# A decoder's closing branch: a hint on every engine ahead of it, the last layer norms inside its arms, the last reload summed by products

## The chip, the core and the metric

The kernel runs on one core of a Trainium2 chip: TensorE (PE, matrix products), VectorE (DVE), ScalarE (ACT), GpSimd (POOL) and SyncE (SP, which issues DMAs), each with its own instruction stream, and 16 DMA engines. The metric is the device time of one execution in microseconds (us). Times within a profile count from the span's first instruction.

## What is computed

Two decoder layers on x (4 batches of 256 tokens, 256 wide), in float32: windowed attention, attention over a context of 1601 rows, a ternary feed-forward, then a second attention, a linear attention, and a mixture of experts. Each step ends in a layer norm of the sum of its input and its outcome. The change lies in the last step:

```python
def _layernorm(x, axis=-1, eps=1e-05):
    m = jnp.mean(x, axis=axis, keepdims=True)
    v = jnp.var(x, axis=axis, keepdims=True)
    return (x - m) / jnp.sqrt(v + eps)
...
        for e in range(E):
            h = jax.nn.silu(x @ w1[e]) * (x @ w3[e])
            out = out + h @ w2[e] * weights[:, e:e + 1]
...
    x = _layernorm(x + _L1_ffn_ref(x, L1_ffn_w_gate, L1_ffn_w1, L1_ffn_w3, L1_ffn_w2), axis=-1)
```

Of the 8 experts each token uses its 2 best, so `weights` has two entries that are not zero in each of the 1024 rows.

## The kernel before, in words

**Order of the work.** The program is written as a graph of operations. A planner (`weave`, L319) walks through it with a cost for each operation and a delay between engines (L192), takes the operation that can start first (ties go by priority, then by order of creation), and so writes out each engine's stream. While `hold_order(True)` is in force (L208), that order is kept; an operation that switches it off leaves the order of its instructions to the scheduler of the language. Buffers come from rings of a fixed number of places, and an operation waits until its ring has one free.

**The experts.** Tokens are entered into lists by expert in DRAM, and the lists are worked off in tiles of 128 rows (`expert_tile`, L1436). SyncE loads the tile's row and its expert from a table `tab` into registers and fetches the rows (`xg`) and two weight matrices (`wt`, a ring of 4). TensorE transposes the rows, multiplies them by both weights (32 products) and by a third (8), and VectorE makes the outcome `ey`. Most tiles are scattered by GpSimd into the table `yd` in DRAM, a row for each token and rank. Tiles are worked off early where the routing so far allows it; 16 late ones are planned after the last routing, with a table of their own (`tile_table`, L1379). It also makes `enough`, a flag in SBUF that says whether 13 late tiles suffice (as they do here), or whether the 3 rare ones are needed too.

**The end.** Four banks in PSUM, `acc[b]`, hold a batch of 256 tokens each. The last two sure tiles aren't scattered: their rows are summed into `acc` by products with a matrix of ones and zeros (`pick`, one piece for each batch, L1504). After the first of the two, the loop at L1653 issues 8 reloads of `yd` (two for each batch, 256 KB each, `back`, a ring of 4 buffers). VectorE adds both to the batch's x (L1660), and TensorE adds x to `acc[b]` by a product with the identity (L1663). Then `norms` (L1514) does for each batch: statistics by VectorE (`st`, `mv`), the power -1/2 by GpSimd (`rstd`), the bias `nmr` and the outcome of the first 128 tokens (`o[:, 0]`) by VectorE. These stand in the planned order.

**The branch.** `end` (L1538) comes behind everything else. Each of the five engines loads `enough` into a register (L1556), and `tc.Switch` (L1557) makes two arms. Arm 1 is `leave` (L1533): ScalarE makes the outcome of the other 128 tokens of each batch and SyncE issues four output DMAs. Arm 0 works off the three rare tiles first, then does the norms again and leaves. Each arm begins with a hint for its own exit, which the language puts there (L1557 in the profile); the jump into the arm and the jump out of it are shown at L1733, as is the closing barrier. All engines but ScalarE and SyncE have nothing to do in arm 1. The loads of L1556 stand outside the kept order.

Of the kernel before, what the change touches and what calls it, by code (L numbers as in the profile page):

```python
# [23 lines left out]
F32 = mybir.dt.float32  # L24
# [22 lines left out]
class View:  # L47
# [138 lines left out]
class Loom:  # L186
# [66 lines left out]
    @contextmanager  # L253
    def piece(self, us, claims=(), ins=(), over=(), what=""):


        self.cur = ([], [], list(ins))
        yield
        fns, outs, ins = self.cur
        self.cur = None  # L260
        if self.at_once is not None:
            over = ()
        read = [o for v in over for _, o in v.buf.reads]
        self.op({"PE": (us, us, lambda: [f() for f in fns])}, outs, ins, claims, after=read, what=what)

    def mm(self, o, lhsT, rhs, start, stop, **kw):
        fns, outs, ins = self.cur
        outs.append(o)
        ins += [v for v in (lhsT, rhs) if isinstance(v, View)]
        fns.append(  # L270
            lambda: self.nc.tensor.matmul(real(o), real(lhsT), real(rhs), start=real(start), stop=stop, **kw)  # L271
        )
# [162 lines left out]
def decoder(ctx: ExitStack, tc: tile.TileContext, a: dict, out: bass.AP):  # L435
    nc = tc.nc
    k = Loom(tc)
    piece, mm, turn = k.piece, k.mm, k.turn


    def scope(side, after=(), on=None):
        s = Scope(k, side, after)
        if on:
            s.opened.deps.add(on.opened)
            on.closed.deps.add(s.closed)
        return s

    base = scope("left")
# [118 lines left out]
    ident = const.tile((P, P), F32, "ident")  # L567
# [43 lines left out]
    vs = []  # L611
    for i in range(2):
        v = p1w.tile((P, 3, H // 2, 2, 32), F32, f"v{i}")
# [624 lines left out]
    LATE = TILES - sum(EARLY)  # L1238
    LAST_TILES = 2
# [271 lines left out]
        k.vector.tensor_tensor(slots, slots, slot, ALU.add)  # L1511
        scatter(yd, slots, y, 1.0, 2.0, "give", cleared)

    def norms(acc):  # L1514

        parts = []
        for b in range(B):
            mv = tiny((P, 2, 2), "mv2")
            for t in range(2):
                st = tiny((P, 6), "st")  # L1520
                k.vector.bn_stats(st, acc[b][:, t, :])
                k.vector.bn_aggr(mv[:, t, :], st)
            rstd = tiny((P, 2), "rstd2")
            k.gpsimd.tensor_scalar(rstd, mv[:, :, 1], 1e-5, None, ALU.add)
            k.gpsimd.tensor_tensor(rstd, rstd, mhalf, ALU.pow)
            nmr = tiny((P, 1), "nmr")
            k.vector.scalar_tensor_tensor(nmr, mv[:, 1, 0:1], -1.0, rstd[:, 1:2], ALU.mult, ALU.mult)
            o = p6.tile((P, 2, D), F32, "back", bufs=4)
            k.vector.tensor_scalar(o[:, 0], acc[b][:, 0], mv[:, 0, 0:1], rstd[:, 0:1], ALU.subtract, ALU.mult)
            parts.append((o, rstd, nmr))  # L1530
        return parts

    def leave(acc, parts):  # L1533
        for b, (o, rstd, nmr) in enumerate(parts):
            k.scalar.activation(o[:, 1], acc[b][:, 1], AF.Identity, scale=rstd[:, 1:2], bias=nmr)
            k.dma_start(out[b * S : (b + 1) * S, :].rearrange("(t p) d -> p t d", p=P), o)

    def end(tiles, tab, enough, level, acc, parts):  # L1538

        spare = {}  # L1540
        for v in (
            p5.tile((P, W), F32, "xg"), p6w.tile((P, 2, 2, EI), F32, "wt"), p6.tile((P, 2, P), F32, "xgT"),
            p6.tile((P, EI // P, P), F32, "eh"), p6.tile((P, D), F32, "ey"), p5.tile((P, 1), F32, "of", bufs=2),
            p6.tile((P, T // P, P), F32, "pick", bufs=LAST_TILES), tiny((P, 2, 2), "mv2"), tiny((P, 6), "st"),
            bank((P, 2, P)), bank((P, EI // P, P)), bank((P, EI // P, P)), bank((P, D)),
        ):
            spare.setdefault(v.buf.group.tag, []).append(v)
        held = [v for vs in spare.values() for v in vs]
        for vs in parts:
            for v, tag in zip(vs, ("back", "rstd2", "nmr")):  # L1550
                spare.setdefault(tag, []).append(v)

        def emit():
            k.hold_order(False)
            engines = (nc.tensor, nc.vector, nc.gpsimd, nc.sync, nc.scalar)
            which = {e.engine: e.value_load(enough.real()[0:1, 0:1], min_val=0, max_val=1) for e in engines}  # L1556
            for arm in tc.Switch(which, 2):  # L1557
                k.at_once = spare
                if arm:
                    leave(acc, parts)  # L1560
                else:
                    for i in tiles:
                        expert_tile(i, tab, level, acc)
                    leave(acc, norms(acc))
                k.at_once = None
            k.hold_order(True)

        outs = [v for vs in parts for v in vs]
        k.op({None: (0.0, 2.5, emit)}, [*acc, *outs], [tab, enough, w2], held, after=[o for o in k.ops if o.bufs], unordered=True)


    for b in range(B):
# [45 lines left out]
    w2 = p6w.tile((P, NE, 4, D), F32, "w2e")  # L1618
    for e in range(NE):
        k.dma_start(w2[:, e], rows(a["w2"][e]))  # L1620
    level = 0
    for b in range(B):
        at_prio(7, b)
        for ts, x, xt in l1_attention(b):
# [5 lines left out]
            if b == B - 1:  # L1630
                at_prio(8)
                n = EARLY[ts[0]]
                tab, taken = tile_table(n, taken)
# [8 lines left out]
    tab, enough = tile_table(LATE, taken, True)  # L1642
    iotaT = p6.tile((P, T), F32, "iotaT", bufs=1)
    iota(iotaT, 1, base=1)
    acc = [bank((P, 2, D)) for _ in range(B)]
    sure = LATE - RARE
    for i in range(sure):
        last = i - sure + LAST_TILES
        if last < 0:
            expert_tile(i, tab, level)  # L1650
        else:
            expert_tile(i, tab, level, acc, last == 0)
        if last == 0:  # L1653
            for b in range(B):
                x = X[b]
                for e in range(2):
                    y = p6.tile((P, 2, D), F32, "back", bufs=4)
                    row0 = 1 + e * T + b * S
                    k.dma_start(y, yd[row0 : row0 + S, :].rearrange("(t p) d -> p t d", p=P))
                    k.vector.tensor_tensor(x, x, y, ALU.add)  # L1660
                with piece(0.87, what="base"):
                    for t in range(2):
                        mm(acc[b][:, t, :], ident, x[:, t, :], False, True, skip_group_check=True)  # L1663
    end(range(sure, LATE), tab, enough, level, acc, norms(acc))
    k.weave()


# [69 lines left out]
```

## Time and profile before

| what | value |
|---|---|
| runs | 687.3, 689.1, 689.75 us (median 689.1) |
| the profiled execution: its time, its span | 687.61 us, 685.9 us |
| TensorE (PE) busy | 653.6 us, 95% |
| VectorE, ScalarE, GpSimd busy | 443.6, 296.2, 121.0 us |
| mean granted TensorE clock | 0.991 |
| DMA | 85.37 MB, mean 124 GB/s |
| first reload issued, last reload issued | 659.36, 665.96 us |
| first output issued, last output issued | 674.34, 678.33 us |

The page gives the busy time of each engine; the timeline gives single instructions, with the idle time ahead of them and what ended it; the view of one source line gives shortest, median and longest of each kind of instruction there, with the first and the last start. A letter q behind an engine means its sequencer, which reads the stream and runs branches, register loads and waits itself. The trace has a record for each of these instructions; where a time below is given to the hundredth for one of them, it is from its record.

### The profile page before, as it was taken

Reading aid. Unit: us, or ns where it says so; the run is one execution under the profiler, and the core shown is the slowest. Engines: PE = TensorE matmul, PEld = TensorE weight load, DVE = VectorE, ACT = ScalarE, POOL = GpSimd, SP = SyncE. Lnnn points to the kernel's source line nnn. Section 1 sums busy time; section 2 is a strip of 40 time slices with the busy share of each in tenths; the row PEclk is TensorE's granted clock in tenths of the full one; section 3 lists DMA queues with packets and bytes.
Section 4 is the critical chain, followed back from the end, with each engine's and each line's share of the span. In section 5 each row is a group of like instructions: output and inputs, shape, how many; then the busy total and the mean of one; then the engine's idle time right before and its main releaser. Section 6 shows DMA issues by size and latency. Waiting matters only on the chain.

```text
span 685.9 us, 12319 instructions
## 1 busy us (share of the span) xinstructions
PE 653.6 (95%) x4389; PEld 521.0 (76%) x4389; DVE 443.6 (65%) x1152; ACT 296.2 (43%) x930; POOL 121.0 (18%) x166
## 2 busy tenths in 40 slices
PE   8999999999999999999999999999997899899992
PEld 6878788678877677777667677777765799899992
DVE  6899886433526845365599997777688466334344
ACT  4779766211132423334346777656455312111101
POOL 3331132122300000000022101141213222121102
PEclk9999999999999999999999999999999999999997
DMA  9932121527998423000010340000000681896442
GB/s 307 357 105 64 46 65 40 177 100 232 328 338 314 158 84 108 0 1 1 0 55 1 105 143 1 1 32 1 31 1 17 209 301 53 298 339 217 147 131 71
DMA packets 62464, 85.37 MB, mean 124 GB/s; under 512 B 4462, under 2 KB 45812, under 8 KB 62388
## 3 DMA queue, kind: packets, MB, share of 16 engines
q1 hardware_dynamic: 60756, 79.96, 35.3%
q0 software_dynamic: 1632, 4.48, 1.8%
q8 instruction: 39, 0.64, 0.4%
q14 instruction: 37, 0.30, 0.1%
HBM read 67.29 MB, written 17.13 MB: 123 GB/s over the span
## 4 chain that ended last, share of the span: by engine, by line
PE 78%; DVE 13%; ACT 4%; DMA 1%; issue 1%; POOL 1%; SPq 0%; DVEq 0%; POOLq 0%; ACTq 0%
PE bank L271 70%; PE bank L278 9%; DVE at L408 3%; ACT at L408 3%; DVE nm L408 2%; DVE x L408 1%; POOL rstd L408 1%; DVE as L408 1%; DVE h L408 1%; DMA wt<-in_w 1%; DVE st L408 1%; DMA back<-yd 1%; DVE entry L408 1%; DVE fm L408 0%; DVE hq L408 0%
## 5 line engine op out<-in xcount | busy, mean ns | idle before, releaser
L408 ACT ACTIVATE at<-at,nm 128x128 f32<-128x128 f32 (+1 forms) x256 | 106.4, 419 | 23.3 <-DVE nm L408 22.6
L271 PE MATMUL bank<-xgT,wt 128*128 128x128 f32 x640 | 75.9, 279 | 1.9 <-DMA wt<-in_w 1.4
L271 PEld LDWEIGHTS bank<-xgT,wt 128*128 128x128 f32 x640 | 75.1, 195 | 3.0 <-issue 1.7
L278 PE MATMUL bank<-ident,at 128*128 128x128 f32 (+1 forms) x440 | 60.8, 275 | 2.0 <-DVE at L408 1.8
L278 PEld LDWEIGHTS bank<-ident,at 128*128 128x128 f32 (+1 forms) x440 | 50.2, 141 | 13.8 <-issue 6.4
L271 PE MATMUL bank<-V,aT 128*128 128x256 f32 (+1 forms) x240 | 55.1, 380 | 0.6 <-DVE o L408 0.6
L271 PE MATMUL bank<-KT,qT 128*128 128x512 f32 (+1 forms) x128 | 54.7, 553 | 0.0
L271 PEld LDWEIGHTS bank<-V,aT 128*128 128x128 f32 (+1 forms) x240 | 45.2, 190 | 10.6 <-issue 3.6
L408 POOL TENSOR_SCALAR rstd<-mv 128x2 f32<-128x2 f32 (+1 forms) x26 | 5.8, 221 | 258.1 <-DVE mv L408 186.9
L271 PE MATMUL bank<-kf,V 128*128 128x256 f32 (+1 forms) x208 | 50.0, 381 | 1.1 <-DVE kf L408 1.1
L408 DVE TENSOR_REDUCE nm<-at 128x4 f32<-128x512 f32 (+1 forms) x64 | 50.6, 808 | 0.4
L271 PE MATMUL bank<-wkv,KT 128*128 128x256 f32 (+1 forms) x208 | 49.6, 382 | 0.0
L408 ACT ACTIVATION_READ_ACCUMULATOR at<-at,nm 128x1 f32 x256 | 48.6, 190 | 0.0
L271 PEld LDWEIGHTS bank<-kf,V 128*128 128x128 f32 (+1 forms) x208 | 38.5, 190 | 7.3 <-DVE kf L408 2.3
L271 PEld LDWEIGHTS bank<-wkv,KT 128*128 128x128 f32 (+1 forms) x208 | 37.9, 186 | 7.0 <-issue 1.0
L408 ACT COPY aT<-bank 128x512 f32<-128x512 f32 (+2 forms) x58 | 30.6, 554 | 26.6 <-PE bank L278 25.8
L408 ACT ACTIVATE eh<-bank 128x512 f32<-128x512 f32 x20 | 11.9, 597 | 68.6 <-PE bank L271 59.0
L408 DVE TENSOR_REDUCE m<-bank 128x1 f32<-128x512 f32 (+1 forms) x32 | 20.4, 639 | 29.7 <-PE bank L271 29.7
L408 DVE TENSOR_TENSOR at<-at,rs 128x512 f32<-128x512 f32 (+1 forms) x44 | 38.4, 872 | 1.0
L408 POOL TENSOR_TENSOR at<-at,rs 128x512 f32<-128x512 f32 (+1 forms) x20 | 22.8, 1142 | 87.5 <-DVE rs L408 80.3
L271 PE MATMUL bank<-w2e,eh 128*128 x160 | 37.8, 380 | 0.0
L408 ACT ACTIVATE fm<-bank 128x512 f32<-128x512 f32 (+2 forms) x33 | 17.9, 550 | 45.7 <-PE bank L271 45.2
(268 smaller groups left out, 1237.0 us busy)
## 6 DMA issues: line engine op xcount, KB each, us to landing
wt<-in_w SPq DMA_DIRECT2D x40, 512.0 KB
lists<-h SPq DMA_DIRECT2D x6, 1548.0 KB
KT<-in_ctxT SPq DMA_DIRECT2D x6, 1024.0 KB
V<-in_ctx SPq DMA_DIRECT2D x6, 1024.0 KB
w2e<-in_w SPq DMA_DIRECT2D x8, 512.0 KB
KT<-in_ctxT SPq DMA_DIRECT2D x6, 577.0 KB
V<-in_ctx SPq DMA_DIRECT2D x6, 512.0 KB
xg<-lists SPq DMA_DIRECT2D x20, 129.0 KB
```

Source lines behind the costliest of these rows:

```text
L271: lambda: self.nc.tensor.matmul(real(o), real(lhsT), real(rhs), start=real(start), stop=stop, **kw)
L278: fns.append(lambda: self.nc.tensor.transpose(real(o), real(x), real(ident)))
L408: return getattr(engine, method)(*[real(x) for x in args], **{k: real(x) for k, x in kw.items()})
```

## The change

There are three parts.

**A hint on every engine.** `tell` is a new operation. It loads `enough` into a register of each engine and issues a hint for the coming branch with it, in the kept order. It is created behind the second-last sure tile and may be planned as soon as that tile has been summed into `acc[0]`; it takes no time in the plan. `end` uses these registers.

**The norms in both arms.** `norms` and `leave` become one function, which both arms call. The statistics of batch b+1 now come ahead of `nmr` and the outcomes of batch b. ScalarE makes seven of the eight outcomes, VectorE the first one of the last batch. `nmr` is made for both halves in one instruction.

**The last reload.** For the last batch, x takes only the first of the two reloads; the second goes to `acc[3]` by products of its own.

```diff
-    def norms(acc):
-
-        parts = []
+    def leave(acc):
+
+        rest = []
+
+        def go(b, mv, rstd):
+            nmr = tiny((P, 2), "nmr")
+            k.vector.scalar_tensor_tensor(nmr, mv[:, :, 0], -1.0, rstd, ALU.mult, ALU.mult)
+            o = p6.tile((P, 2, D), F32, "back", bufs=4)
+            for t in range(2):
+                if t == 0 and b == B - 1:
+                    k.vector.tensor_scalar(o[:, t], acc[b][:, t], mv[:, t, 0:1], rstd[:, t : t + 1], ALU.subtract, ALU.mult)
+                else:
+                    k.scalar.activation(o[:, t], acc[b][:, t], AF.Identity, scale=rstd[:, t : t + 1], bias=nmr[:, t : t + 1])
+            k.dma_start(out[b * S : (b + 1) * S, :].rearrange("(t p) d -> p t d", p=P), o)
+
...
             k.gpsimd.tensor_tensor(rstd, rstd, mhalf, ALU.pow)
...
+            rest.append((b, mv, rstd))
+            if b:
+                go(*rest.pop(0))
+        go(*rest.pop(0))
+
+    def ask(enough):
+
+        engines = (nc.tensor, nc.vector, nc.gpsimd, nc.sync, nc.scalar)
+        return {e.engine: e.value_load(enough.real()[0:1, 0:1], min_val=0, max_val=1) for e in engines}
+
+    where = {}
+
+    def tell(enough, what):
+
+        def emit():
+            where.update(ask(enough))
+            tc.switch_hint(where, 2, "end")
+
+        k.op({None: (0.0, 0.1, emit)}, [], [enough, what], unordered=True)
...
         def emit():
             k.hold_order(False)
-            engines = (nc.tensor, nc.vector, nc.gpsimd, nc.sync, nc.scalar)
-            which = {e.engine: e.value_load(enough.real()[0:1, 0:1], min_val=0, max_val=1) for e in engines}
-            for arm in tc.Switch(which, 2):
+            for arm in tc.Switch(where, 2, "end"):
                 k.at_once = spare
-                if arm:
-                    leave(acc, parts)
-                else:
+                if not arm:
                     for i in tiles:
                         expert_tile(i, tab, level, acc)
-                    leave(acc, norms(acc))
+                leave(acc)
...
         if last == 0:
+            tell(enough, acc[0])
             for b in range(B):
                 x = X[b]
                 for e in range(2):
                     y = p6.tile((P, 2, D), F32, "back", bufs=4)
...
-                    k.vector.tensor_tensor(x, x, y, ALU.add)
-                with piece(0.87, what="base"):
-                    for t in range(2):
-                        mm(acc[b][:, t, :], ident, x[:, t, :], False, True, skip_group_check=True)
-    end(range(sure, LATE), tab, enough, level, acc, norms(acc))
+                    if e == 0 or b < B - 1:
+                        k.vector.tensor_tensor(x, x, y, ALU.add)
+                for v in (x,) if b < B - 1 else (x, y):
+                    with piece(0.87, what="base"):
+                        for t in range(2):
+                            mm(acc[b][:, t, :], ident, v[:, t, :], False, True, skip_group_check=True)
+    end(range(sure, LATE), tab, enough, level, acc)
```

More of the change, by code (lines that the diff above doesn't have):

```diff
@@ L1525, in norms, with end @@
             k.gpsimd.tensor_tensor(rstd, rstd, mhalf, ALU.pow)
[L1526 to L1538, printed above, removed]
+            rest.append((b, mv, rstd))
[11 more added lines that the diff above has]
+        k.op({None: (0.0, 0.1, emit)}, [], [enough, what], unordered=True)
+    def end(tiles, tab, enough, level, acc):
         spare = {}
@@ L1543, in end @@
             p6.tile((P, EI // P, P), F32, "eh"), p6.tile((P, D), F32, "ey"), p5.tile((P, 1), F32, "of", bufs=2),
-            p6.tile((P, T // P, P), F32, "pick", bufs=LAST_TILES), tiny((P, 2, 2), "mv2"), tiny((P, 6), "st"),
+            p6.tile((P, T // P, P), F32, "pick", bufs=LAST_TILES),
+            *[tiny((P, 2, 2), "mv2") for _ in range(4)], *[tiny((P, 6), "st") for _ in range(4)],
+            *[tiny((P, 2), "rstd2") for _ in range(4)], *[tiny((P, 2), "nmr") for _ in range(4)],
+            *[p6.tile((P, 2, D), F32, "back", bufs=4) for _ in range(4)],
             bank((P, 2, P)), bank((P, EI // P, P)), bank((P, EI // P, P)), bank((P, D)),
@@ L1548, in end @@
         held = [v for vs in spare.values() for v in vs]
-        for vs in parts:
-            for v, tag in zip(vs, ("back", "rstd2", "nmr")):
-                spare.setdefault(tag, []).append(v)
         def emit():
             k.hold_order(False)
-            engines = (nc.tensor, nc.vector, nc.gpsimd, nc.sync, nc.scalar)
-            which = {e.engine: e.value_load(enough.real()[0:1, 0:1], min_val=0, max_val=1) for e in engines}
-            for arm in tc.Switch(which, 2):
+            for arm in tc.Switch(where, 2, "end"):
                 k.at_once = spare
-                if arm:
-                    leave(acc, parts)
-                else:
+                if not arm:
                     for i in tiles:
                         expert_tile(i, tab, level, acc)
-                    leave(acc, norms(acc))
+                leave(acc)
                 k.at_once = None
             k.hold_order(True)
-        outs = [v for vs in parts for v in vs]
-        k.op({None: (0.0, 2.5, emit)}, [*acc, *outs], [tab, enough, w2], held, after=[o for o in k.ops if o.bufs], unordered=True)
+        k.op({None: (0.0, 2.5, emit)}, acc, [tab, enough, w2], held, after=[o for o in k.ops if o.bufs], unordered=True)
     for b in range(B):
```

## The prediction

> **What bounds the kernel now.** I read the page's chain first: TensorE holds 78% of the path to the end, VectorE 13%. The change touches only the last 27 us and one register load, so I went on to the branch's own records, the timeline of the tail, and the chain around that load.
>
> The records of the end of the program (min/median/max in ns, first and last start in us):
>
> ```profile
> L1733 SPq DRAIN  x3: 7/7/13, 681.2 to 685.3; - x3
> L1733 POOLq DRAIN  x3: 40/113/2927, 682.1 to 685.6; - x3
> L1733 ACTq COMPARE_BRANCH  x2: 43/50/58, 657.7 to 677.8; - x2
> ...
> L1733 PEldq COMPARE_BRANCH  x2: 3435/3989/4543, 671.1 to 675.0; - x2
> ...
> L1733 POOLq COMPARE_BRANCH  x2: 43/56/70, 676.5 to 679.5; - x2
> ...
> L1733 DVEq COMPARE_BRANCH  x2: 60/68/75, 677.3 to 680.4; - x2
> L1733 ACTq DRAIN  x2: 14/78/142, 678.2 to 685.3; - x2
> ...
> L1733 DVEq DRAIN  x2: 10/29/48, 683.0 to 685.4; - x2
> ```
>
> Each engine branches twice, into its arm and out of it. The arm's first instruction is this one:
>
> ```profile
> L1557 ACTq BRANCH_PREFETCH_HINT  x1: 46/46/46, 660.2 to 660.2; - x1
> ...
> L1557 POOLq BRANCH_PREFETCH_HINT  x1: 52/52/52, 679.3 to 679.3; - x1
> ...
> L1557 DVEq BRANCH_PREFETCH_HINT  x1: 61/61/61, 680.2 to 680.2; - x1
> ```
>
> GpSimd branches at 676.45 and is in its arm at 679.31: 2.86 us. It leaves at 679.50 and drains at 682.12: 2.62 us more. Its DRAIN then lasts 2.93 us, to 685.05, and the closing barrier starts from there and ends the span 0.8 us later. VectorE pays 2.93 and 2.53 us in the same way. ScalarE, which reached its arm at 660, leaves at 677.75 and drains at 678.20, so an exit hinted long before costs 0.45 us. SyncE has seen the last output land by 681.0 and drains at 681.25. So **two branches and a drain on an engine with no work left** end the program, 3.8 us after the data are out.
>
> The tail's own work (timeline, start and duration in us):
>
> ```profile
> 671.97 1.89 PE L271 MATMUL bank<-ey,pick 128*128 128x256 f32 x8
> ...
> 674.34 4.36 SPq L285 DMA_DIRECT2D out<-back  x4
> ...
> 677.04 0.16 DVE L408 SCALAR_TENSOR_TENSOR nmr<-mv,rstd 128x1 f32<-128x1 f32 x1 [0.37 <-POOL rstd L408]
> 677.12 0.54 DVE L408 TENSOR_SCALAR back<-bank,mv,rstd 128x256 f32<-128x256 f32 x1
> 677.74 0.56 ACT L408 ACTIVATE back<-bank,nmr,rstd 128x256 f32<-128x256 f32 x1 [0.42 <-DVE back L408]
> ```
>
> The last product ends at 673.86, the last outcome at 678.30; the last output is issued at 678.33 and lands by 681.0.
>
> Last, the chain of waits around the loads of `enough` (start, us, what):
>
> ```profile
> 581.54 0.55 DVEq L1556
> 582.09 0.08 issue
> 582.16 0.22 DVEq L1556
> ...
> 582.57 0.48 DVE ey L408
> ```
>
> ```profile
> 585.41 4.63 DMA wt<-in_w
> 590.04 0.14 issue
> 590.18 3.81 PE bank L271 x32
> ```
>
> Today's register loads were placed early in the instruction order, right behind `enough`. VectorE's stands in front of the outcome `ey`, which stands in front of `tab`, and SyncE needs `tab` to ask for the first late weights. No transfer runs until 585.4, and TensorE idles 1.36 us for them at 590.18.
>
> [...]
>
> **The change part by part.** Numbers are against the profiled execution (687.61 us, span 685.9).
>
> *Moving the loads.* The five loads leave the place above. VectorE's there is five waits, load, arithmetic and assert, 581.05 to 582.50. Without it `ey` starts when its products end (581.57) and the step before allows: 581.65, as `rowi` follows the same kind of step by 0.60 at 575.63. That is 582.57 - 581.65 = 0.9 us earlier for `tab`, SyncE's requests and the first weights, whose queue is empty till then. TensorE's idle 1.36 us covers it. From 594.7 on TensorE runs without a wait on transfers, so the gain stays. **-0.9 us**; bounds -1.36 (the whole idle time) and 0 (another input of that tile is late next).
>
> *The hint, with the loads in front of it.* The planner puts `tell` when the second-last sure tile has been summed into acc[0]. By the planned times of before that is behind VectorE's first reload sum, behind SyncE's first four reload issues, behind TensorE's second summing piece of that tile, and behind all other work of ScalarE and GpSimd. ScalarE and GpSimd wait there for 10 us, so it is free on them. SyncE issues its fourth reload by 661.3 and its fifth at 663.88, when the first buffer comes free: 2.6 us, against 0.54 for a load and its check (579.12 to 579.66) and some 0.3 for the hint: free. TensorE's sequencer is 2.7 us ahead of its array (branch read at 671.14, last product ends 673.86) and takes a 0.63 us load (592.71 to 593.34) without a gap: free; with that cover gone, 0.6. On VectorE it is not free. The sequencer starts at 663.19; the load with its waits is 1.45 us, the hint, an unseen form, is taken as a branch set-up (0.3 at 677.06 to 677.36) with its own 0.06: 1.8 us, to 665.0. The second sum could start at 663.88, so sums two to four are 1.1 us late (0.65 if the five waits go). Behind them queue the sixth to eighth reload, whose buffers they free, and TensorE's sums. The fifth, issued in time, no longer shares the rings, so I take **+0.6 us** for the products; bounds 0.2 and 1.1.
>
> *The last reload by products.* VectorE loses one sum (0.67 us, no longer last); TensorE gains one piece of four matmuls at 0.216 us, 0.86 us. By priority both pieces for b=3 now stand ahead of the last tile's sums for b=1 to 3. From the b=2 piece at 669.27: b=3 at 670.24 and 671.10, then summing at 671.97, 672.83 and 673.69. acc[1] is complete at 673.0 (before: 671.3), acc[3] at 674.7 (673.9).
>
> *The norms in the arm.* VectorE ends its sums at about 669.8 and dispatches. If the arm is there, it starts at 670.4 (+0.6) and norms b=0 before acc[1] is complete. One batch is 0.95 us of statistics (674.85 to 675.80); then GpSimd starts 0.2 later and takes 1.0 (676.00 to 677.01). Statistics of b=1 at 673.03, of b=2 at 674.05; nmr of b=1 waits for GpSimd till 675.22; statistics of b=3 from 675.30 to 676.25; GpSimd 676.45 to 677.46; nmr at 677.49, before 677.04. The outcome on VectorE and the one on ScalarE then need 0.56 side by side if ScalarE waits for nmr alone (end 678.25), or one after the other, as at 677.12 and 677.74 (end 678.75). Output issued at 678.3 to 678.75, before 678.33: 0 to +0.4, I take **+0.2 us**. ScalarE's seven at 0.56 fit in its 1.1 us per batch.
>
> *Leaving the arms.* GpSimd enters its arm while idle, hinted or not, and hints its exit 10 us ahead. After its last power at 678.06 (677.46 + 0.6) it should drain after 0.45, as ScalarE did, at 678.5; with the same 2.93, done at 681.4. VectorE is out by 680. TensorE has no work in the arm: even at its 4.54 it is in time. So the end goes to the output: SyncE's drain at 681.25 + 0.6 + 0.2 = 682.05, and the barrier follows. The slack of 685.05 - 681.25 = 3.8 is gone: **-3.8 us**. What is late next is the landing, with GpSimd's drain 0.65 us behind; without that cover each further 0.1 on GpSimd counts.
>
> **Sum:** -0.9 + 0.6 + 0.2 - 3.8 = -3.9 us. The span becomes 682.0, the profiled execution 683.7. It lies 1.5 below the median of 689.1, so I put the same 3.9 on the median: **685.2 us**. Its own range, from the bounds, is 684.2 to 686.6.
>
> **Rivals.** (B) *Cheaper:* five waits are dropped on VectorE and ScalarE waits for nmr alone: 0.2 and 0 in place of 0.6 and 0.2, so 684.6, or 684.1 with the whole idle time saved. For it: 0.9 us of cover before acc[1]. (C) *The exits still fetch:* GpSimd is done at 678.06, fetches 2.62 and drains 2.93: 683.6, against 685.05: -1.4 - 0.9 = -2.3, **686.8**. Against it: ScalarE's 0.45. (D) *The hint into the arm does nothing*, so the change doesn't do what it says: VectorE's arm starts at 673.9 and the statistics of b=1 at 674.9. GpSimd's power for b=0 then ends at 676.05 and holds nmr and the statistics of b=2 behind it; those of b=3 start at 677.27, nmr of b=3 at 679.4 in place of 678.1: +1.3, **686.5**. For it: no hint of this kind, from a register, is in the trace. (E) *Slower:* [...] At TensorE's dearest 4.54 us: 4.54 on the reload path and 4.54 - 2.2 at the arm, 6.9 in all: -3.9 + 6.9 = +3.0, **692.1**. [...] against it: about a dozen VectorE instructions lie between hint and branch.
>
> **How the numbers follow.** Forecast 0.55, B 0.14, C 0.11, D 0.15, E 0.05. Runs of before spread by 2.45 us, so I widen the outer cases by 1: 683.1 to 687.9. A measurement of this kernel tells about 0.5% (3.4 us, 685.7) from no change. Two thirds of the forecast, nearly all of B and a fifth of D lie below: faster 0.53; same 0.42; slower 0.05, from E.
>
> **What would show it.** After the change: no L1556-like load before `ey` near 581, and the first wt wait of TensorE 0.9 shorter; VectorE's hint into the arm within 0.5 us of its branch; GpSimd's drain starting below 679; SyncE's drain the last before the barrier, at about 682. A branch of VectorE or GpSimd followed by 2.5 us of nothing is D or C; a pause of that length between reload sums is E; GpSimd's long drain ending last would make the sum wrong.

## The result, and the profile after

| | before | after | after, measured again |
|---|---|---|---|
| median of the runs | 689.75 us | 687.11 us | 687.78 us (before beside it: 689.95) |
| lowest to highest | 687.3 to 690.98 | 684.19 to 687.74 | 684.75 to 689.08 |
| ratio to before, 95% interval | | 0.9956 (0.9938 to 0.9975) | 0.9970 (0.9952 to 0.9988) |
| profiled execution: time, span | 687.61, 685.9 us | 684.19, 682.4 us | span 685.5 us |

The change makes the kernel faster, by 2.6 us the first time and 2.2 the second, 0.4 and 0.3%. Predicted were 3.9 us. The profiled execution, against which the sum was made, gained 3.42 us in time and 3.52 in span (685.90 - 682.38). So there are two questions: whether the terms behind those 3.5 us are the predicted ones, and why the medians show about 1 us less.

**The end of the program.** In the kernel after, the loads of `enough` are at L1546, the hint for the branch at L1554, each arm's hint for its own exit at L1575, and the jumps and the closing barrier at L1751. The view of that last line (shortest/median/longest in ns, first and last start in us):

```profile
L1751 POOLq DRAIN  x3: 40/113/3190, 677.0 to 682.1; - x3
L1751 SPq DRAIN  x3: 7/7/13, 681.5 to 681.8; - x3
...
L1751 POOLq COMPARE_BRANCH  x2: 56/62/68, 655.6 to 676.5; - x2
...
L1751 DVEq COMPARE_BRANCH  x2: 63/73/83, 668.4 to 677.3; - x2
...
L1751 PEldq COMPARE_BRANCH  x2: 364/1833/3302, 669.9 to 674.0; - x2
...
L1751 DVEq DRAIN  x2: 19/54/90, 677.9 to 681.8; - x2
```

GpSimd leaves its arm at 676.53 and starts its long DRAIN at 676.97: 0.44 us, where it took 2.62. That DRAIN is as long as ever (3.19 us), but it is over at 680.16. SyncE has seen the last output land at 681.50, and the span ends 0.88 later. The end has gone from an idle engine to the output, as the sum said.

**The entries.** The hints for the branch, and the first instruction of each arm:

```profile
L1554 PEldq BRANCH_PREFETCH_HINT  x1: 53/53/53, 661.7 to 661.7; - x1
L1554 SPq BRANCH_PREFETCH_HINT  x1: 45/45/45, 661.7 to 661.7; - x1
...
L1554 DVEq BRANCH_PREFETCH_HINT  x1: 68/68/68, 663.8 to 663.8; - x1
```

```profile
L1575 SPq BRANCH_PREFETCH_HINT  x1: 36/36/36, 669.8 to 669.8; - x1
L1575 PEldq BRANCH_PREFETCH_HINT  x1: 36/36/36, 670.3 to 670.3; - x1
L1575 DVEq BRANCH_PREFETCH_HINT  x1: 45/45/45, 671.3 to 671.3; - x1
```

VectorE jumps at 668.36 and is in its arm at 671.27: 2.91 us, as without a hint (2.93). SyncE takes 3.20, ScalarE 3.27, GpSimd 2.81. TensorE alone jumps at 669.89 and is there at 670.32. **On four of five engines the hint into the arm saved nothing.** GpSimd's stands at 580.69, ahead of fourteen scatters; the prediction had put it behind all of that engine's other work. ScalarE's comes 0.26 us ahead of the jump, and there the jump even took longer: 3.2 to 3.3 us in the four profiles with this lead, 2.5 to 2.7 in the six with no hint or with a missed one 3.7 us or more ahead. ScalarE has 12 us to wait after it, so this costs nothing.

The prediction and the expectations speak of fetches. What a jump waits for isn't shown: while VectorE jumps (668.36 to 671.27), packets of the two instruction queues start at 669.40, 670.38 (8 KB each) and 671.02 (16 KB), but their records name no engine, so taking one for VectorE's, or for the cause of its wait, is a guess.

**The late weights.** What TensorE waited for between 575 and 600 us (total, times, longest), first from the list of before, then the whole list of after:

```profile
PE bank L271 <- DMA wt<-in_w: 1.4, 1, 1.4
```

```profile
PE bank L271 <- DVE xgT L408: 0.5, 1, 0.5
```

**The tail** (timeline: start and duration in us, idle time before in brackets):

```profile
663.97 2.62 DVE L408 TENSOR_TENSOR entry<-entry,back 128x512 f32<-128x512 f32 x4 [1.22 <-DMA back<-yd]
...
670.89 2.75 PE L271 MATMUL bank<-ey,pick 128*128 128x256 f32 x12
671.43 0.43 DVE L408 BATCH_NORM_STATS2 st<-bank 128x6 f32<-128x256 f32 x1 [2.61 <-PE bank L271]
...
675.09 3.96 SPq L285 DMA_DIRECT2D out<-back  x4
...
677.31 0.16 DVE L408 SCALAR_TENSOR_TENSOR nmr<-mv,rstd 128x2 f32<-128x2 f32 x1 [0.97 <-POOL rstd L408]
677.39 0.54 DVE L408 TENSOR_SCALAR back<-bank,mv,rstd 128x256 f32<-128x256 f32 x1
678.09 0.56 ACT L408 ACTIVATE back<-bank,nmr,rstd 128x256 f32<-128x256 f32 x1 [0.69 <-SPq L1751]
```

The 1.22 us ahead of the second sum hold the loads and the hint (VectorE's sequencer is at them from 661.95 to 663.85); the list puts them down to the reload, which had landed. The 2.61 ahead of the first statistics are put down to TensorE, but acc[0] had long been complete: they are the jump. These busy rows show no jump; the sequencer's records have it, at 668.36 and 671.27.

**An account that doesn't depend on the execution.** Executions differ by several us ahead of the tail, so I count the tail from the start of the last sure tile's outcome `ey` on VectorE. "Landing" is the time from the issue of the last output to SyncE's drain. All in us, one profile each. The two profiles of the kernel after differ by 0.27 in the last output and by 0.54 in the end, so a difference between two rows that is smaller than this says little by itself.

| kernel | `ey` at | VectorE jumps | is in its arm | last output issued | landing | end |
|---|---|---|---|---|---|---|
| before | 662.77 | 14.53 | 17.46 | 15.56 | 2.86 | 23.13 |
| after | 661.66 | 6.69 | 9.61 | 17.01 | 2.82 | 20.71 |
| after, again | 664.25 | 6.65 | 9.86 | 17.28 | 3.09 | 21.25 |
| e1 no hint | 662.67 | 6.24 | 9.34 | 16.83 | 4.27 | 22.01 |
| e2 loads moved alone | 661.93 | 14.58 | 17.81 | 15.61 | 3.43 | 24.66 |
| e3 norms in the arms alone | 667.13 | 6.87 | 9.99 | 17.35 | 3.78 | 22.04 |
| e4 hint 7 us earlier | 664.90 | 5.94 | 9.04 | 16.46 | 3.68 | 21.03 |
| e5 hint 81 us ahead | 664.56 | 6.79 | 7.39 | 16.27 | 3.40 | 20.56 |
| e6 hint 61 us ahead | 663.62 | 6.12 | 6.72 | 15.74 | 3.20 | 19.83 |
| e7 last reload summed | 665.81 | 7.23 | 10.17 | 17.51 | 2.94 | 21.35 |
| e8 last outcome split | 663.41 | 6.39 | 9.25 | 16.64 | 3.09 | 20.62 |
| e9a hint 22 us ahead | 662.97 | 5.62 | 8.71 | 16.10 | 3.52 | 20.49 |
| e9b hint 20 us ahead | 662.38 | 6.50 | 9.65 | 17.07 | 3.26 | 21.21 |
| e12 e6, order held | 662.20 | 5.86 | 6.46 | 15.17 | 4.15 | 20.20 |

The records of the granted TensorE clock fit most of the differences in `ey`. Between 300 and 600 us TensorE ran at full clock but for stretches of 3.4 us at half of it, in which it had work, and their number is not the same in each execution. With one stretch (before, after, e1, e2, e9a, e9b, e12) `ey` stands at 661.7 to 663.0, with two (after again, e4, e5, e6, e8) at 663.4 to 664.9, with three (e3, e7) at 665.8 and 667.1. Half of 3.4 us is 1.7 us lost for each, by estimate. The profiled executions of before and after have one each, so they can be compared.

For the profiled executions: `ey` is 1.1 us earlier, the last output comes 1.45 us later after it, the landing is the same, and from SyncE's drain to the end it is 0.88 in place of 4.71. Together -1.10 + 1.45 - 0.04 - 3.83 = -3.52.

### The profile page after: what moved, and what is told of

Read it like the earlier page. It is cut to its first block, busy times and chain, and to the rows that moved or that the text cites. A ratio compares the mean times of both kernels' runs of the same rounds, so it can differ in the third digit from the quotient of the medians.

```text
span 682.4 us, 12346 instructions
## 1 busy us (share of the span) xinstructions
PE 654.6 (96%) x4389; PEld 521.1 (76%) x4393; DVE 442.3 (65%) x1148; ACT 297.5 (44%) x933; POOL 121.1 (18%) x166
## 4 chain that ended last, share of the span: by engine, by line
PE 66%; DVE 14%; issue 11%; ACT 4%; POOL 3%; DMA 1%; DVEq 0%; POOLq 0%; SPq 0%; ACTq 0%
PE bank L271 57%; PE bank L278 8%; DVE at L408 4%; ACT at L408 3%; DVE nm L408 2%; POOL yd L1290 2%; DVE x L408 1%; DVE as L408 1%; DVE h L408 1%; DVE st L408 1%; DMA back<-yd 1%; POOL rstd L408 1%; DVE entry L408 0%; DVE fm L408 0%; DMA yd<-ey,slots 0%
## 5 line engine op out<-in xcount | busy, mean ns | idle before, releaser
L271 PE MATMUL bank<-xgT,wt 128*128 128x128 f32 x640 | 74.3, 275 | 0.7 <-DVE xgT L408 0.5
L271 PEld LDWEIGHTS bank<-xgT,wt 128*128 128x128 f32 x640 | 73.5, 192 | 1.8 <-DVE xgT L408 0.8
L408 POOL TENSOR_TENSOR at<-at,rs 128x512 f32<-128x512 f32 (+1 forms) x20 | 22.8, 1141 | 87.6 <-DVE rs L408 80.4
```

The costliest lines, as they stand in the source:

```text
L408: return getattr(engine, method)(*[real(x) for x in args], **{k: real(x) for k, x in kw.items()})
```

## The experiments

My theory after the result: moving the loads gives 1.1, the exits give 3.8, and 1.5 is given back because VectorE's arm is late and its norms are slower than planned; the hints, but for TensorE's, save nothing. Times below are medians, and each ratio is to the kernel before measured beside it. All kernels compute everything.

### The parts alone

**e1: no hint.**

```diff
-            tc.switch_hint(where, 2, "end")
...
-            for arm in tc.Switch(where, 2, "end"):
+            for arm in tc.Switch(where, 2):
```

> The kernel after without its hint; the five register loads stay at their new place. Theory (of the five entry hints only TensorE's does anything, and TensorE's jump is hidden): VectorE's jump into the arm still takes 2.8 us, TensorE's takes 3.4 to 4.5 us instead of 0.36 and moves nothing; VectorE's stop between the first two reload sums is 0.45 us shorter, which the landing of the sixth reload absorbs; outputs and the last drain within 0.3 us of the kernel after in a profile at the same clock (span 682.1 to 682.5 at a granted clock of 0.993), times equal within the interval. Rival (the hints help VectorE or SyncE, or TensorE's late jump holds the end): the last output is issued at least 0.8 us later, span 683.2 or more.

Measured: 687.11 us, ratio 0.9965 (0.9951 to 0.9979); the kernel after had 687.11. VectorE's jump took 3.10, TensorE's 3.75 into the arm and 4.56 out of it. The span (684.7) misses what I had written and would fit the rival, but only because `ey` came 1.0 us later and the landing took 4.27; after `ey` the last output is issued 0.2 us *earlier* than with the hint. So no gain is seen from the hint where the change puts it, and TensorE's jump, the one that it saves, is hidden. An expectation in absolute times was a mistake: from here on I read the tail from `ey`.

**e2: the loads moved, nothing else.**

```diff
+            tell(enough, acc[0])
...
-            which = {e.engine: e.value_load(enough.real()[0:1, 0:1], min_val=0, max_val=1) for e in engines}
-            for arm in tc.Switch(which, 2):
+            for arm in tc.Switch(where, 2):
```

(`tell` holds the five loads here, and no hint.)

> The kernel before with one edit: the five register loads are issued in the kept order, behind the second-last sure tile's first summing. No hint, norms ahead of the branch as before. Theory (the move is worth 1.1 us and nothing else): the wait of TensorE for its first late weights is 1.1 us shorter than before, the jump out of the arms stays as it was (GpSimd's drain starts 2.6 us after its jump and ends last): span 684.8 against 685.9 at a clock of 0.991. Rival (the gain of the move is given back in the tail, by the loads on VectorE between the reload sums): the wait shortens but the last output and the span are at most 0.5 us earlier.

Measured: 689.44 us, ratio 1.0000 (0.9982 to 1.0018), and a span of 686.6 us, 1.8 above the expected one. TensorE's first late weights, which waited 1.36 us before:

```profile
589.34 3.81 PE L271 MATMUL bank<-xgT,wt 128*128 128x128 f32 x32 [0.49 <-DMA wt<-in_w]
```

The wait is 0.87 shorter and `ey` 0.84 earlier; the last output stands where it stood after `ey` (15.61 against 15.56), so the rival's way of giving it back isn't seen. The end is 1.5 later after `ey`, since GpSimd's jump into the arm took 3.76 and its exit 3.21 here, against 2.86 and 2.62. The theory holds for the wait, not for the span. In the time no gain is seen; the interval of 1.2 us to either side would hide it, and GpSimd's two jumps took 5.48 us together before and 6.97 here.

**e3: the norms in both arms, nothing else** (the loads stay at 581, no hint, eight sums by VectorE).

> The kernel before with the norms moved into both arms and nothing else: loads stay near 581, no hint, eight reload sums by VectorE. Theory (the norms in the arm give VectorE and GpSimd 6 us between arm entry and exit[...]): GpSimd and VectorE drain within 0.5 us of their jump out, GpSimd's drain ends before SyncE's, the end is SyncE's drain, 3.8 us off the exits; the outputs come 1.5 to 2.2 us later (late arm 0.6 to 0.9, outcomes in series 0.57, the eighth sum 0.6 of VectorE ahead of its jump): span 683.4 to 684.2 at 0.991. Rival (the early hint does it: the exits are late without it): drains 2.5 us after the jump, span 686 or more.

Its diff is that of `leave` and `end` in the change, without `tell`. Measured: 689.58 us, ratio 0.9986 (0.9970 to 1.0002). Its drains:

```profile
L1748 POOLq DRAIN  x3: 45/118/3176, 682.9 to 688.9; - x3
L1748 SPq DRAIN  x3: 7/7/13, 688.3 to 688.6; - x3
```

GpSimd drains 0.46 us after its jump (682.40 to 682.85) and is done at 686.03, 2.2 us ahead of SyncE's drain. The rival falls: with work in the arm GpSimd's exit took 0.46 us, and the hint at L1554 has no part in it. TensorE has no work in either arm and so hints its exit only 0.41 us ahead; its jump out still takes 4.80 us here. The outputs come 1.79 later after `ey`, as expected; the end comes 1.09 earlier and not 1.7 to 2.5, because the landing took 3.78. The interval of the time just includes no change at all, so this part shows in the profile only.

**e7: the last reload summed by VectorE.**

```diff
-                    if e == 0 or b < B - 1:
-                        k.vector.tensor_tensor(x, x, y, ALU.add)
-                for v in (x,) if b < B - 1 else (x, y):
-                    with piece(0.87, what="base"):
-                        for t in range(2):
-                            mm(acc[b][:, t, :], ident, v[:, t, :], False, True, skip_group_check=True)
+                    k.vector.tensor_tensor(x, x, y, ALU.add)
+                with piece(0.87, what="base"):
+                    for t in range(2):
+                        mm(acc[b][:, t, :], ident, x[:, t, :], False, True, skip_group_check=True)
```

> The kernel after with its third part undone: VectorE sums the eighth reload too, TensorE has one piece of base products less. Theory (the eighth sum stands ahead of VectorE's jump and so delays its whole arm by 0.6 to 0.7 us and by the wait for the eighth landing; TensorE is not the limit): the last output is issued 17.6 to 18.2 us after the last sure tile's outcome instead of 17.0, the end 0.6 to 1.2 us later. Rival (TensorE's extra piece costs as much as the sum it replaces, since acc[3] is complete 0.9 us later): no difference, within 0.2 us.

Measured: 687.15 us, ratio 0.9967 (0.9955 to 0.9978). VectorE jumps 0.5 us later, the output is issued at 17.51 in place of 17.01 and 17.28. So the third part is worth 0.2 to 0.5 in the profile, less than I expected, and nothing that the time shows.

### Why the hint does nothing, and what a working one would give

**e4: loads and hint some 7 us earlier.**

```diff
+        if last == 0:
+            tell(enough, [o for o in k.ops if o.what == "tensor_tensor"][-1])
...
-            tell(enough, acc[0])
```

(Here and in e5, e6, e9a and e9b, `tell` waits for the named operation instead of acc[0].)

> The kernel after with loads and hint planned some 7 us earlier, behind VectorE's last addition of row numbers of the tile before; VectorE's hint is then about 11 us ahead of its jump, SyncE's 12, ScalarE's 7. Theory H1 (a hint works when it is given at least about 6 us ahead, as the exits show at 6.06): VectorE is in its arm within 0.5 us of its jump, SyncE too, statistics of the first batch start 1 to 2 us earlier, the last output is issued 0.5 to 0.9 us earlier, span 681.5 to 681.9 at 0.993. Theory H2 (a hint with its target in a register does nothing on these engines[...]): VectorE's jump still costs 2.5 to 2.9 us, the last output is where it was, span 682.1 to 682.5.

Measured: 687.07 us, ratio 0.9962 (0.9949 to 0.9975). VectorE's hint came 10.5 us ahead and its jump still took 3.10: H1 falls. But SyncE's hint had moved up to 583.87, and SyncE was in its arm after 0.52: a hint from a register does work, so H2 falls as well, for SyncE. What the two differ in, the engine aside, is the lead (84.8 us against 10.5) and how much code lies between hint and jump.

**e5 and e6: the hint far ahead.**

```diff
+        if i == 0:
+            tell(enough, [o for o in k.ops if o.what == "tensor_copy"][-1])
```

```diff
+        if i == 2:
+            tell(enough, [o for o in k.ops if o.what == "tensor_tensor"][-2])
```

> The kernel after with loads and hint of VectorE, TensorE, ScalarE and SyncE planned some 70 us earlier, behind the copy of the first late tile's rows (VectorE's hint at about 590, behind the table's last step, so that the late weights are not delayed). Theory H3 (outside TensorE a hint is only acted on if it comes before the engine has entered the block of code that holds the branch; VectorE's last block fetch before the branch is the one at 598.7, some 128 instructions ahead of the arm; SyncE's hint at 584 in the run before worked, VectorE's 10.5 us ahead of its jump did not): VectorE and SyncE are in their arms within 0.5 us of the jump, no fetch follows VectorE's jump, its first statistics start some 2.3 us earlier, the last output is issued 15.9 to 16.3 us after the last sure tile's outcome instead of 17.0. Rival H2 (hints from a register do nothing on VectorE at any distance): its jump takes 2.8 us again, 17.0 us stays.

> The same with loads and hint behind the third late tile's product of the two halves (VectorE's hint at about 607, behind the fetch at 598.7 but still 60 us ahead of the jump). Theory H3 (block, not lead, decides): VectorE's jump takes 2.8 us as in the kernel after. Rival H1b (a hint needs a long lead, more than the 10.5 us tried): VectorE is in its arm within 0.5 us.

Measured: e5 685.40 us, ratio 0.9937 (0.9914 to 0.9961); e6 685.27 us in its one run. In both VectorE is in its arm 0.60 after the jump, ScalarE 0.47, SyncE 0.52. VectorE's records in e6 (first start of the first line, then the second):

```profile
L1752 DVEq COMPARE_BRANCH  x2: 63/73/83, 669.7 to 678.0; - x2
```

```profile
L1575 DVEq BRANCH_PREFETCH_HINT  x1: 45/45/45, 670.3 to 670.3; - x1
```

e6's statistics, where the kernel after has 2.61 us of idle time ahead of the first:

```profile
670.50 0.43 DVE L408 BATCH_NORM_STATS2 st<-bank 128x6 f32<-128x256 f32 x1 [0.30 <-issue]
...
673.27 0.43 DVE L408 BATCH_NORM_STATS2 st<-bank 128x6 f32<-128x256 f32 x1 [1.59 <-PE bank L271]
```

Now VectorE waits for acc[1] (the second line), and that wait is real. e5, which jumps as late as the kernel after (6.79 and 6.69), issues its last output at 16.27: the late arm cost **0.74 us** against the first profile of the kernel after, 1.01 against the second. e5's time is lower than that of the kernel after, but the intervals of their ratios overlap (0.9914 to 0.9961 against 0.9938 to 0.9975), so it does not show the gain. For e6 I had expected, with H3, a jump of 2.8 us; it came out as the rival H1b, a long lead, had it. H3's place was wrong, since e6's hint stands behind the fetch that I had named (an 8 KB packet of an instruction queue, at 598.72 in the kernel after) and still works.

**e9a and e9b: the limit from below** (`if i == 9`, with `[-2]` and `[-1]` of the additions).

> The kernel after with VectorE's loads and hint some 24 us ahead of its jump, so that the hint is about its 1209th recorded instruction. In every run so far VectorE's last block fetch before the branch falls at its instruction 1215, wherever the hint stands; hints at 1238 (4.6 us ahead) and 1231 (10.5 us ahead) did nothing, hints some 50 and 100 instructions ahead of 1215 worked. Theory H3, with the place corrected (the hint must come before that fetch): VectorE is in its arm within 0.7 us of the jump. Rival H1b (the hint needs a long lead, somewhere between 10.5 and 61 us): undecided here, read together with the next run.

> The same with the hint one step later, some 19 us ahead of the jump, at VectorE's instruction 1217 or so, just behind the fetch. H3: the jump takes 2.6 to 3.1 us again, although the lead is nearly twice the one of 10.5 us. H1b: hit in both or miss in both unless its limit happens to lie between 19 and 24 us; a hit here ends H3.

Measured: both missed; VectorE's jumps took 3.09 and 3.16. e9a's hint turned out to stand just behind the instruction that the supposed fetch follows, and not some six ahead of it, so it doesn't test what it was made for. Their times, 685.19 and 685.31 us in one run each, are as short as e6's 685.27, so a single run says nothing here on what a hint is worth. All hints into the arm together, by the lead in us and the time from jump to arm:

| engine | missed | worked |
|---|---|---|
| VectorE | 4.5 to 5.4, 10.5, 19.6, 22.2 (2.9 to 3.2 us) | 61, 81 (0.60) |
| ScalarE | 0.3, 3.7, 11.6 (2.5 to 3.3) | 52, 69, 76 (0.47) |
| SyncE | 4.6 to 5.1 (3.2) | 56, 77, 85, 86 (0.52) |
| TensorE | | 8.1 to 83 (0.42) |
| GpSimd | 75 to 76 (2.6 to 2.9) | |

The lead in time could be the rule for each engine by itself (H1b): on VectorE the limit would lie between 22.2 and 61 us. It would not be the same for every hint, since the hint for the exit, each arm's first instruction, was obeyed on VectorE with 6.06 us (the jump out took 0.56); but that hint is of another form: no register loads stand ahead of it at L1575, as they do at L1554. The register alone is not the reason: the same form works at 61. The other candidate is the place in the code. By VectorE's records, counted from 0, hints at 1141 and 1163 worked, hints from 1215 to 1238 did not. In the kernel after an 8 KB packet of an instruction queue starts at 654.01, 1.09 us behind record 1214 (652.92); H3 took it for VectorE's, which its record doesn't say. A hint that has to come before it is the author's conjecture, and no run separates place from lead: between records 1163 and 1215, which are also 61 and 22.2 us ahead, nothing was tried. GpSimd's hint (31 instructions and 75 us ahead, never obeyed) fits neither. This cause is **open**.

### The last outcome, and the best version

**e8: the last batch's outcomes in tiles and DMAs of their own.**

```diff
+            if b == B - 1:
+                half = p6.tile((P, D), F32, "half", bufs=1)
+                k.vector.tensor_scalar(half, acc[b][:, 0], mv[:, 0, 0:1], rstd[:, 0:1], ALU.subtract, ALU.mult)
+                k.scalar.activation(o[:, 1], acc[b][:, 1], AF.Identity, scale=rstd[:, 1:2], bias=nmr[:, 1:2])
+                k.dma_start(out[b * S : b * S + P, :], half)
+                k.dma_start(out[b * S + P : (b + 1) * S, :], o[:, 1], engine="ACT")
+                return
```

> The kernel after with one edit in its norms: the two outcomes of the last batch are in tiles of their own and go out by a DMA each, VectorE's by SyncE and ScalarE's by ScalarE's own queue. Theory (in the kernel after ScalarE waits 0.57 us for VectorE's outcome because both write one tile, so the two are done one after the other on the path that sets the end): ScalarE's last outcome starts with VectorE's, the later of the two DMAs is issued about 0.6 us earlier (16.4 us after the last sure tile's outcome instead of 17.0), span 0.6 less at the same landing. Rival (ScalarE's issue or its queue is slower than SyncE's): the outcome is earlier and the landing is not.

Measured: 686.08 us, ratio 0.9957 (0.9939 to 0.9975). Its last outcomes:

```profile
678.76 0.54 DVE L408 TENSOR_SCALAR half<-bank,mv,rstd 128x256 f32<-128x256 f32 x1
...
679.34 0.34 SPq L285 DMA_DIRECT2D out<-half  x1
679.46 0.56 ACT L408 ACTIVATE back<-bank,nmr,rstd 128x256 f32<-128x256 f32 x1 [0.70 <-issue]
680.05 0.39 ACTq L285 DMA_DIRECT2D out<-back  x1
```

ScalarE still waits for VectorE's outcome, so a tile of its own is not enough, and the series stays. The records show that `nmr` gives no signal of its own here; VectorE's signal comes with the outcome behind it, at 679.31, and ScalarE's wait ends at 679.33. In the kernel after this is not so: `nmr` signals at 677.48, and ScalarE waits on to 677.96, just behind the outcome's signal at 677.94. Whether the shared tile is what holds it there, e8 therefore doesn't tell. (The later DMA is issued at 16.64, but 0.3 of the gain on 17.01 is VectorE's earlier jump, 6.39 against 6.69.) The two outcomes read the same bank; whether that is why they are put in series wasn't tried. The cause is open.

**e12: e6, with the order held in the arms.**

```diff
+            sts = [tiny((P, 6), "st") for t in range(2)]
             for t in range(2):
-                st = tiny((P, 6), "st")
-                k.vector.bn_stats(st, acc[b][:, t, :])
-                k.vector.bn_aggr(mv[:, t, :], st)
+                k.vector.bn_stats(sts[t], acc[b][:, t, :])
+            for t in range(2):
+                k.vector.bn_aggr(mv[:, t, :], sts[t])
...
+                k.hold_order(True)
                 leave(acc)
+                k.hold_order(False)
```

> The kernel of the hint at 607 us (behind the third late tile's product) with the order of the norms held in the arms: both statistics of a batch, then both aggregates, where the language's scheduler had put an aggregate behind each. Theory: VectorE needs 0.95 to 1.0 us a batch instead of 1.15 and is the limit from acc[1] to the last aggregate, so the last output is issued 15.1 to 15.5 us after the last sure tile's outcome (15.7 without, 17.0 in the kernel after); against the kernel after 1.5 to 1.9 us less, time 685.2 to 685.7 where the kernel after has 687.1. Rival (TensorE's last product, some 11.5 us after that outcome, is the limit): 15.6 to 15.8.

Measured: 686.67 us, ratio 0.9953 (0.9937 to 0.9969). A batch in pairs:

```profile
671.70 0.77 DVE L408 BATCH_NORM_STATS2 st<-bank 128x6 f32<-128x256 f32 x2 [1.90 <-PE bank L271]
672.37 0.30 DVE L408 BATCH_NORM_AGGREGATE mv<-st 128x2 f32<-128x6 f32 x2
672.59 0.13 DVE L408 SCALAR_TENSOR_TENSOR nmr<-mv,rstd 128x2 f32<-128x2 f32 x1
672.64 0.76 DVE L408 BATCH_NORM_STATS2 st<-bank 128x6 f32<-128x256 f32 x2
```

From batch 1 to batch 2 it takes 0.94 us, in e6 1.15 (673.27 to 674.42). The last output is issued at 15.17 as expected, 0.57 earlier than in e6 and 1.84 earlier than in the kernel after. Of the 0.57, 0.15 are there before the new order can act, since the statistics of batch 1, which wait for TensorE, start 9.50 us after `ey` and not 9.65; the order is worth the other 0.42. The time is 1.1 us below that of the kernel after beside it (687.78), less than the 1.5 to 1.9 expected, and the intervals of the two ratios overlap; the landing of the profiled execution was 4.15. e5 and e12 have the lowest medians of several runs, but these runs tell them neither from each other nor surely from the kernel after.

**The kernel after, again.**

> The kernel after once more. Theory (the profiled execution of the first job was the lowest of nine, with a landing of the last output of 2.8 us, where seven other profiles of kernels that end on that landing have 2.9 to 4.3): time 686.5 to 687.3, its profile a span of 683 to 685.5 with a landing above 3 us, the last output issued 16.8 to 17.2 us after the last sure tile's outcome. Rival (the first profile is typical and the other runs were slow for another reason): a span of 682.2 to 682.8 again.

Measured: 687.78 us, a little above the range that I gave; last output at 17.28, span 685.5, landing 3.09. The first profile, with span 682.4, was not typical: this one has two stretches at half clock where the first had one, which by the estimate above is 1.7 of the 3.1 us between them.

## Why the prediction was right, and where it was not

687.1 lies in the range, 1.9 above the likeliest time, and 687.8 just inside it. The range held in part because it was laid around the rivals B to D: C's 686.8 and D's 686.5 are nearer to the result than the forecast's 685.2, and the time alone would speak for them. By the prediction's own line at 685.7 the result falls on the side of "same", to which it gave 0.42, though the interval of the ratio excludes no change. Its range from the bounds was also summed wrongly: they give 684.1 to 686.8, not 684.2 to 686.6. Step by step:

- **The loads, -0.9.** Right: -1.1 in the profile of after, -0.84 in e2. The wait of 1.36 is gone in the kernel after; 0.3 to 0.5 of it remained in e1, e2 and e4. A stretch that holds this wait and little else, from the last outcome `ey` ahead of it to the first behind it, takes 11.5 us in the two kernels with the loads at the old place (before and e3) and 9.9 to 10.7 in the twelve profiles with them moved.
- **The loads on VectorE ahead of the sums, +0.6.** The stop was sized well (1.1 said, 1.19 measured at the second sum), its effect was not: the sixth sum starts 5.79 us after `ey`, before 5.76. The sixth reload, issued late, landed in 2.67 us in place of 3.83. The products were no later for it: 0.0. I had bounded this at 0.2 from below, too high.
- **"VectorE ends its sums at about 669.8 and dispatches. If the arm is there, it starts at 670.4."** This step failed. The arm wasn't there: VectorE jumped at 668.36 and was in it at 671.27. The hint did nothing, which is rival D with D's own sign, 2.5 us of nothing behind VectorE's branch; it cost 0.74 us (e5) in place of D's 1.3. On VectorE, ScalarE, SyncE and GpSimd the entries took 2.5 to 3.3 us in all profiles where a hint was missed. I had only an exit's hint to go by, ScalarE's 0.45 us, and that one came 17.5 us ahead and as the first instruction of its arm. Why the hint for the entry was missed stays open.
- **Order of norms and last outcome, +0.2.** Too small. The outcomes run in series (nmr at 677.31, end at 678.65), the upper end that I had named. And I took 0.95 us a batch from a stream in a kept order; in the arm, where that order is off, an aggregate follows each statistics and a batch takes 1.15 (e6). Keeping the order brought 0.42 (e12 against e6). With the 0.74 this is 1.16 of the 1.45 us by which the output is later, where +0.8 had been predicted; the rest is about the size of what two profiles of one kernel differ by.
- **The exits, -3.8.** Right: 4.71 to 0.88 us from SyncE's drain to the end, -3.83; GpSimd and VectorE drain 0.44 and 0.56 after their jumps. e3 shows that the norms in the arm alone do it. Rival C falls with this, and E too: no pause of 2.5 us stands between the sums, the longest is 1.22.
- **What is late next.** I wrote that the end goes to the landing, and took the landing from one execution, 2.86 us, where it had 3.8 us of cover. Now it ends the program, and in the twelve profiles of kernels that end on it, it took 2.8 to 4.3 us, 3.4 in the mean. That is 0.6 that the profile of after (2.82) doesn't show and the medians should: 3.5 - 0.6 = 2.9, against 2.6 and 2.2 measured. The remaining 0.3 to 0.7 lie within the intervals. This part is worked out from the profiles, not shown by a run of its own; a somewhat different number of half-clock stretches in the runs behind the medians would do as much.

Of the 3.9 predicted, then, 0.65 were lost to the later output (1.45 against 0.8), some 0.6 perhaps to the landing, and the exits and the loads gave what they should.

## What to carry to other kernels

Work in the arm made its exit cheap here (on GpSimd 0.44 us in place of 2.62): it puts time between the exit's hint and the jump. On VectorE 6.0 us were enough, the 0.2 of the empty arm were not, and between them nothing was tried. A hint for the entry has to be seen to work in the jump's own record, and here VectorE's missed at 22 us ahead and worked at 61, for a reason that stays open; loads and hint can stand that early, if nothing that another engine waits for stands behind them. When a change uncovers a transfer, price the transfer by its spread over several executions, and when a step moves to where the order isn't kept, price it at the order that it will get.

## What was not expected of the hardware

- TensorE's hint out of its arm, 3.67 us ahead of the jump, saved only a part: the jump took 3.36 us, and in e1 with 0.42 us ahead 4.56. In all profiles it took 3.1 to 4.1 us with a lead of 2.7 to 3.9 and 4.6 to 5.1 with 0.4. Its hint into the arm, 8.2 us ahead, left 0.42.
- A missed jump has no fixed price: on GpSimd 2.6 to 3.8 us over these kernels, on TensorE 3.4 to 5.1.
- GpSimd's closing DRAIN took 2.93 to 3.19 us on an engine that had done its last operation, in all fourteen profiles; the other engines' took 0.01 to 0.17.
- The mean granted clock counts the end, where TensorE has no work. The columns ahead of the last two are the clock of the stretch, in the kernel before and then after:

```profile
676.00:680.00 4.00, 0.00 (x0) 0.00 (x0) 1.23 (x4) 1.13 (x2) 0.93 (x3) 0.64 0.64 205
```

```profile
676.00:680.00 4.00, 0.00 (x0) 0.00 (x0) 0.95 (x4) 1.73 (x4) 1.07 (x3) 0.59 0.72 235
```

  TensorE's last product ends at 673.9 and 673.6, and the clock then falls to half, at 677.1 and 676.7, until the end. That is 8.8 us before and 5.7 after. The kernel after has a higher mean over its runs (0.991 against 0.989). The shorter end accounts for that, 3.1 us at half clock being 0.002 of the span; it is no sign that its products run faster.
